# Spatial attention: one product of q and k over the places for both images of a pair

## The chip, the cores and the metric

The kernel runs on one core of a Trainium2 chip. A core has a matrix engine (TensorE), a vector engine (VectorE), a scalar engine (ScalarE), a general engine (GpSimd) and a queue processor (SyncE), which run beside each other and wait for each other by semaphores. The trace calls them PE, DVE, ACT, POOL and SP; PEld is TensorE's loading of weights, PE its matmuls. SBUF is the working memory of 128 partitions, PSUM the memory in which TensorE adds up its products. The metric is the device time of one execution in microseconds (us), lower is better.

## The reference, cut to what matters

The whole program is two layers on an image batch: a convolutional block with an attention in frequency and one in space, then a state space layer. The change concerns the spatial attention of the first layer:

```python
B, DIM, HEADS, H, W = (8, 128, 8, 128, 128)
...
q_s = qkv(q1_w, q1_b, q3_w, q5_w).reshape(b, HEADS, hd, h * w)
k_s = qkv(k1_w, k1_b, k3_w, k5_w).reshape(b, HEADS, hd, h * w)
v_s = qkv(v1_w, v1_b, v3_w, v5_w).reshape(b, HEADS, hd, h * w)
q_s = _l2norm_lastdim(q_s)
k_s = _l2norm_lastdim(k_s)
attn_s = jnp.einsum('bhcn,bhdn->bhcd', q_s, k_s) * temp_s[None]
attn_s = jax.nn.softmax(attn_s, axis=-1)
out_s = jnp.einsum('bhcd,bhdn->bhcn', attn_s, v_s).reshape(b, c, h, w)
```

Here qkv is a 1x1 convolution followed by grouped 3x3 and 5x5 convolutions. For each image and each of 8 heads, every one of 16 channels of q is multiplied with every one of 16 channels of k and summed over all 16384 places. That sum, before the norms, is what the change makes in another way.

## The kernel before, in words

The program runs in stages. First come group norm and the 1x1 convolutions, then the attention in frequency, then the spatial attention (lines 505 to 602), then a stage that mixes both (from line 610), and last the state space layer. Everything is in fp32.

The stage of the spatial attention takes the eight images in four pairs (loop over b, line 559). An image's channels are cut in four blocks (loop over blk, line 562), and each block holds 16 groups; a group is one step of the grouped convolutions.

conv (line 517) loads one quad of groups of both images into src (one of three buffers, issued from SyncE's queue, line 521) and makes it with 64 products of 32 by 32 weights by 512 columns into four PSUM tiles c_mm (line 529). What happens to a c_mm tile is decided by the function that is handed in. use_q squares it on ScalarE and writes it on VectorE twice into qm, once for each of two kinds of channels, with the other kind's partitions zeroed (lines 544 and 545). use_k squares it and copies it into kk (line 549). use_v copies it to vst and stores it.

qm has the shape 128 x (kind 2) x (group 16) x (image 2) x (place 256), and kk the shape 128 x (group 16) x (image 2) x (place 256). The partitions hold the position in an 8 by 8 patch and the channel of the group, and the last axis holds the patches. So neighbouring groups, read at one place, lie 512 words apart, and neighbouring images 256 words apart.

After the twelve calls of conv for q, v and k of a block comes the sum over the places. For each of the two images f, 256 products are made, one for each place n: the weights are 32 columns of qm (2 kinds by 16 groups), the moving data 16 columns of kk, both contracted over the 128 partitions. Product n goes to the PSUM partitions 32 j to 32 j + 31 with j = n modulo 4, so four partial sums run beside each other in the four column groups of the array. VectorE copies them out (gs, line 579), and one product with the constant sums4 adds the four partial sums into at (the tile c_at, line 581). Two further products (line 583) put the sums of squares beside it. qm, kk, the PSUM tile c_gram and the PSUM tile c_at have one buffer each.

Then conv makes the fourth kind, the convolution of x itself, for the block's groups (line 585), and the next block follows. After the four blocks the norms and the softmax of both images are worked out on VectorE and ScalarE (from line 586).

The order on each engine is set by a scheduler when the program is built. On TensorE it stands like this in a block: the 256 products of the first image, four products of the next conv, the one c_at product from gs and the two from sq, the 256 products of the second image, again four products of conv, the three c_at products, and then the rest of conv. In the trace every fp32 product shows as two pairs of a weight load and a matmul.

small is a constant of 128 columns, of which the first 82 are used. Its first 32 columns are sums4, and line 516 names its parts.

Of the kernel before, what the change touches and what calls it, by code (L numbers as in the profile page):

```python
# [9 lines left out]
F32 = mybir.dt.float32  # L10
# [8 lines left out]
NH, HD = 8, 16  # L19
# [26 lines left out]
def _constants():  # L46
    i = np.arange(128)
    ang = 2 * np.pi * np.outer(i, i) / 128
    cos, sin = np.cos(ang), np.sin(ang)
    block = (i[:, None] // HD == i[None, :] // HD).astype(np.float64)  # L50
    u = np.arange(1, 64)

    tc = np.concatenate([cos[:, 64:65], sin[:, u], cos[:, u], cos[:, 0:1]], 1)
    a1 = np.concatenate([cos[64:65], 2 * sin[u], 2 * cos[u], cos[0:1]], 0) / HW
    a2 = np.concatenate([cos[64:65], 2 * cos[u], -2 * sin[u], cos[0:1]], 0) / HW
    made = {
        "ident": np.eye(128),
        "group4": (i[:, None] // 4 == i[None, :] // 4) / 4.0,
        "mask": block,
        "neg": (block - 1) * 1e30,  # L60

        "c16": block * np.cos(2 * np.pi * np.outer(i, i) / HD) / HD,
        "s16": block * np.sin(2 * np.pi * np.outer(i, i) / HD) / HD,
        "first": block * (i[None, :] % HD == 0) / HD,

        "cmp": cos.reshape(128, 32, 4).transpose(0, 2, 1).reshape(128, 128),
        "smp": sin.reshape(128, 32, 4).transpose(0, 2, 1).reshape(128, 128),
        "tc": tc, "cm": cos, "sm": sin, "sneg": -sin, "a1": a1, "a2": a2,
    }


    kind, quarter = i // 16 % 2, i // 32
    made["blocks"] = (kind[:, None] == i[None, :] // 64) & (quarter[:, None] == i[None, :] // 16 % 4)
    small = np.zeros((128, 128))
    small[:, 0:32] = i[:, None] % 32 == i[None, :32]
    small[:, 32:64] = kind[:, None] == i[None, :32] // 16
    small[:, 64:80] = i[:, None] % 16 == i[None, :16]
    small[:, 80:82] = kind[:, None] == i[None, :2]
    made["small"] = small

    ker = np.exp(2j * np.pi * np.outer(np.arange(HW), i) / HW).mean(1)
    ker = ker[(128 * (i[None, None, :] - i[:, None, None]) + i[None, :, None]) % HW]
    ker = np.stack([-ker.imag, ker.real, ker.imag], 2)
    return (
        np.concatenate([made[n] for n in _CONSTS], 1).astype(np.float32),
        ker.astype(np.float32),
    )
# [6 lines left out]
def _layout(a):  # L94

    a = {n: np.asarray(v) for n, v in a.items()}
    o = {"x": np.ascontiguousarray(a["x"]).reshape(B, C, HW)}
    o["consts"], o["ker"] = _constants()
    p = "L0_conv_"
    f, s = a[p + "projf_w"].reshape(C, 2 * C), a[p + "projs_w"].reshape(C, 2 * C)  # L100
# [67 lines left out]
def tile_kernel(ctx: ExitStack, tc: tile.TileContext, I: dict, out: bass.AP):  # L168
    nc = tc.nc
# [25 lines left out]
    def const(name, n=1):  # L195
        i = _CONSTS.index(name)
        return cst[:, i * 128 : (i + n) * 128]
# [60 lines left out]
    with tc.tile_pool(name="a_x", bufs=4) as xp_, tc.tile_pool(name="a_p", bufs=5) as pp_, tc.tile_pool(  # L258
        name="a_t", bufs=2
# [3 lines left out]
        for b in range(B):  # L263
# [67 lines left out]
            for i in range(HW // px):  # L331
# [5 lines left out]
                n = rows if i else rows - 1  # L337
# [21 lines left out]
    with tc.tile_pool(name="b_x", bufs=1) as xp_, tc.tile_pool(name="b_g", bufs=1) as gp_, tc.tile_pool(  # L359
        name="b_w", bufs=3  # L360
# [18 lines left out]
        for b in range(B):  # L379
# [7 lines left out]
            for q in range(2):  # L387
# [10 lines left out]
                for k in range(4):  # L398
                    kk = 4 * q + k
# [6 lines left out]
            for u in range(5):  # L406
# [4 lines left out]
                for c0 in range(0, 13 * C, 512):  # L411
                    n = min(512, 13 * C - c0)
# [5 lines left out]
            gram = psum.tile([128, 512], F32, name="f_gram", tag="ps")  # L418
            for d in (1, 0):
# [5 lines left out]
                for v in range(64):  # L425
                    nc.tensor.matmul(  # L426
                        gram[:, :128], lhsT=xh[:, :, (W - 64 * d - v) % W], rhs=xr[:, :, v],
                        start=(d == 1 and v == 0), stop=(d == 0 and v == 63),
# [76 lines left out]
    with tc.tile_pool(name="c_w", bufs=1) as cw_, tc.tile_pool(name="c_qk", bufs=1) as qkp, tc.tile_pool(  # L505
        name="c_x", bufs=3
    ) as srcp, tc.tile_pool(name="c_v", bufs=6) as vp_, tc.tile_pool(name="c_s", bufs=2) as sp_, tc.tile_pool(
        name="c_ps", bufs=6, space=PSUM
# [4 lines left out]
                taps[:, 4 * i : 4 * i + 4].rearrange("p g c o m -> p (g c o m)"), I["taps"][:, i * 2048 : (i + 1) * 2048]  # L513
            )
        small = const("small")
        sums4, kinds, same16, ofkind = small[:, 0:32], small[:, 32:64], small[:, 64:80], small[:, 80:82]
        def conv(b, cv, gq, use):

            src = srcp.tile([128, 2, PL], F32, name="src")
            for f in range(2):  # L520
                nc.sync.dma_start(src[:, f, :], PQKVX[cv][b + f, 8 * gq : 8 * gq + 8].rearrange("c n s -> (c n) s"))
            grid = src.rearrange("p f (i j) -> p f i j", j=GR)
            banks = [psum.tile([128, 2, 256], F32, name="c_mm", tag="ps") for _ in range(4)]
            for o in range(4):
                for r in range(4):
                    rs = slice(32 * r, 32 * r + 32)
                    for s in range(4):
                        y0, x0 = 8 * s + o // 2, o % 2
                        nc.tensor.matmul(  # L529
                            banks[r][32 * s : 32 * s + 32].rearrange("p f (i j) -> p f i j", j=32),  # L530
                            lhsT=taps[rs, gq, cv, o, :], rhs=grid[rs, :, y0 : y0 + 8, x0 : x0 + 32],
                            start=(o == 0), stop=(o == 3),
                        )
            for r in range(4):
                use(cv, 4 * gq + r, banks[r])
# [23 lines left out]
        for b in range(0, B, 2):  # L559
            sq = sp_.tile([128, 2, 2, NG], F32, name="sq")  # L560
            at = gps_.tile([128, 2, 3, HD], F32, name="c_at")
            for blk in range(4):

                qm = qkp.tile([128, 2, HD, 2, 256], F32, name="qm")
                kk = qkp.tile([128, HD, 2, 256], F32, name="kk")
                for gq in range(4 * blk, 4 * blk + 4):
                    for cv, use in ((0, use_q), (2, use_v), (1, use_k)):
                        conv(b, cv, gq, use)
                for f in range(2):

                    gram = gps_.tile([128, HD], F32, name="c_gram")
                    for n in range(256):
                        j = n % 4
                        nc.tensor.matmul(  # L574
                            gram[32 * j : 32 * j + 32, :], lhsT=qm[:, :, :, f, n].rearrange("p a g -> p (a g)"),
                            rhs=kk[:, :, f, n], start=(n < 4), stop=(n >= 252),
                        )
                    gs = sp_.tile([128, HD], F32, name="gs")
                    nc.vector.tensor_copy(gs, gram)
                    js, gb = slice(32 * blk, 32 * blk + 32), slice(HD * blk, HD * blk + HD)  # L580
                    nc.tensor.matmul(at[js, f, 0], lhsT=sums4, rhs=gs, start=True, stop=True)
                    for n in range(2):
                        nc.tensor.matmul(at[js, f, 1 + n], lhsT=kinds, rhs=sq[:, f, n, gb], start=True, stop=True)
                for gq in range(4 * blk, 4 * blk + 4):
                    conv(b, 3, gq, use_v)
            for f in range(2):

                rn = sp_.tile([128, 2, HD], F32, name="rn")
                nc.scalar.activation(rn, at[:, f, 1:3], AF.Sqrt)
                nc.vector.tensor_scalar(rn, rn, L2_EPS, None, ALU.max)  # L590
                nc.vector.reciprocal(rn, rn)
                rq = sp_.tile([128, 1], F32, name="rq")
                nc.vector.tensor_tensor(rn[:, 0], rn[:, 0], same16, ALU.mult)
                nc.vector.tensor_reduce(rq, rn[:, 0], AX.X, ALU.add)
                a = sp_.tile([128, HD], F32, name="at_a")
                nc.vector.tensor_tensor(a, at[:, f, 0], rn[:, 1], ALU.mult)
                nc.vector.tensor_scalar(a, a, rq, cvec[:, 4:5], ALU.mult, ALU.mult)
                mx = sp_.tile([128, 1], F32, name="at_m")
                nc.vector.tensor_reduce(mx, a, AX.X, ALU.max, negate=True)
                sm = sp_.tile([128, 1], F32, name="at_sum")  # L600
                nc.scalar.activation(a, a, AF.Exp, bias=mx, accum_out=sm)
                nc.vector.reciprocal(sm, sm)
                nc.vector.tensor_scalar(aS[:, b + f, :], a, sm, None, ALU.mult)
# [6 lines left out]
    with tc.tile_pool(name="d_o", bufs=1) as op_, tc.tile_pool(name="d_v", bufs=2) as vp_, tc.tile_pool(  # L610
        name="d_k", bufs=3
    ) as kp, tc.tile_pool(
        name="d_w", bufs=3
# [3 lines left out]
        for b in range(B):  # L617
# [43 lines left out]
            n = H // RB  # L661
# [49 lines left out]
    with tc.tile_pool(name="e_c", bufs=1) as cp, tc.tile_pool(name="e_w", bufs=2) as wk, tc.tile_pool(  # L711
        name="e_h", bufs=4
    ) as hp, tc.tile_pool(name="e_d", bufs=3, space=DRAM) as dp, tc.tile_pool(
        name="e_b", bufs=2, space=PSUM
# [337 lines left out]
        for n in range(-2 * ST, (total + 1) * ST):  # L1052
            i, s = divmod(n, ST)
# [40 lines left out]
```

## The time and the profile before

| what | value |
|---|---|
| time, median of 3 runs | 21334.16 us (21333.18 to 21354.21) |
| time of the profiled execution | 21360.55 us |
| its span, first to last instruction | 21358.5 us |
| mean granted TensorE clock | 0.945 |
| PE busy in the span | 18573.9 us (87%) |
| DVE busy in the span | 13875.6 us (65%) |
| c_gram matmuls (line 574) | x16384, busy 450.6 us, 258 ns each |
| c_gram weight loads (line 574) | x16384, busy 442.6 us, 215 ns each |
| c_mm matmuls (line 529) | x32768, busy 1522.0 us, 657 ns each |
| gs copies (line 579) | x32, 174 ns each |

Engines overlap, so busy times do not add up to the span. The duration of a single matmul or load is a latency: many are in flight at once, and how often one starts is read from a count in a window of time. The chain of waits follows the work that ended last back through what released it, and shows which work lay on the path. An "issue" piece in it is time in which an engine waited for nothing that the profile shows. A row of a window gives the stretch, its length, then for each engine the busy time and the number of instructions, then the granted clock, the busy share of the DMA engines and GB/s.

### The profile page before, as it was taken

Reading aid. Unit: us, or ns where it says so; the run is one execution under the profiler, and the core shown is the slowest. Engines: PE = TensorE matmul, PEld = TensorE weight load, DVE = VectorE, ACT = ScalarE, POOL = GpSimd, SP = SyncE. Lnnn points to the kernel's source line nnn. Section 1 sums busy time; section 2 is a strip of 40 time slices with the busy share of each in tenths; the row PEclk is TensorE's granted clock in tenths of the full one; section 3 lists DMA queues with packets and bytes.
Section 4 is the critical chain, followed back from the end, with each engine's and each line's share of the span. In section 5 each row is a group of like instructions: output and inputs, shape, how many; then the busy total and the mean of one; then the engine's idle time right before and its main releaser. Section 6 shows DMA issues by size and latency. Waiting matters only on the chain.

```text
span 21358.5 us, 802425 instructions
## 1 busy us (share of the span) xinstructions
PE 18573.9 (87%) x360816; PEld 10741.9 (50%) x360816; DVE 13875.6 (65%) x14884; ACT 11748.4 (55%) x25436; POOL 11924.1 (56%) x7116
## 2 busy tenths in 40 slices
PE   5647889889998898988989999898998989989898
PEld 3335667644546565644444444444444444444444
DVE  3332111133332333379999999999999999999999
ACT  2222222222222221267777777777777777777777
POOL 2221000000001111178889889898888888989888
PEclk8878999988889999999999999999999999999999
DMA  9996333255557888854444444444444444444443
GB/s 275 277 278 171 82 82 77 67 201 195 194 193 218 235 228 237 226 109 97 94 102 96 99 97 95 103 96 100 95 95 101 96 100 96 98 101 96 103 96 84
DMA packets 2989828, 2929.13 MB, mean 137 GB/s; under 512 B 1480494, under 2 KB 2275630, under 8 KB 2981667
## 3 DMA queue, kind: packets, MB, share of 16 engines
q1 hardware_dynamic: 2274818, 2537.53, 46.9%
q10 hardware_dynamic: 672672, 206.02, 4.5%
q0 software_dynamic: 38912, 134.24, 2.0%
q8 instruction: 2842, 46.56, 0.9%
q14 instruction: 584, 4.78, 0.1%
HBM read 1975.21 MB, written 902.04 MB: 135 GB/s over the span
## 4 chain that ended last, share of the span: by engine, by line
PE 53%; DVE 19%; ACT 12%; DMA 8%; issue 6%; SPq 2%; POOL 1%; DVEq 0%; ACTq 0%; POOLq 0%
DVE hs L157 14%; PE hb L157 9%; PE c_mm L529 6%; PE y L157 4%; PE e_xc L157 4%; ACT dA L157 4%; ACT L157 4%; DVE bd L157 3%; DMA d_ls<-LS 2%; PE e_z L157 2%; PE x_q L471 2%; PE d_a L641 2%; PE f_gram L426 2%; PE c_gram L574 2%; PE a_mm L308 2%
## 5 line engine op out<-in xcount | busy, mean ns | idle before, releaser
L157 POOL TENSOR_TENSOR hc<-hs,crep 128x1024 f32<-128x1024 f32 x4096 | 9648.7, 2374 | 1308.3 <-DVE hs L157 808.1
L157 DVE TENSOR_TENSOR_SCAN hs<-dA,state,hb 128x512 f32<-128x512 f32 x7936 | 9584.5, 1263 | 854.3 <-PE hb L157 788.4
L157 PEld LDWEIGHTS hb<-bd,duT 64*32 64x32 f32 x262144 | 3749.3, 106 | 3751.0 <-issue 2769.6
L157 PE MATMUL hb<-bd,duT 64*32 64x128 f32 x262144 | 4925.4, 275 | 727.8 <-issue 507.7
L157 ACT ACTIVATE dA<-dlrep,A 128x512 f32<-128x512 f32 x8192 | 5443.4, 713 | 6.9 <-ACT state L157 0.8
L157 PE MATMUL e_xc<-u,wf 128*128 128x512 f32 x4096 | 2255.5, 644 | 412.1 <-ACT u L157 365.4
L656 POOL TENSOR_TENSOR sq<-sq 128x512 f32<-128x512 f32 x256 | 324.5, 1268 | 3269.8 <-ACT sq L655 3269.8
L157 PE MATMUL y<-hc,gath 128*32 128x512 f32 x16384 | 2090.2, 611 | 12.9 <-issue 11.4
L157 ACT COPY state<-hs 128x2 f32<-128x2 f32 x4096 | 776.6, 190 | 1903.4 <-DVE hs L157 1885.5
L529 PE MATMUL c_mm<-src,taps 32*32 32x512 f32 x32768 | 1522.0, 657 | 168.9 <-ACT junk L540 74.7
L157 ACT ACT_TABLE_LOAD x1023 | 1312.5, 1283 | 346.1 <-PE e_dt L157 287.6
L493 POOL DMA_DIRECT2D OFL<-ya x128 | 113.6, 887 | 2448.2 <-ACT ya L490 2448.2
L529 PEld LDWEIGHTS c_mm<-src,taps 32*32 32x32 f32 x32768 | 636.0, 107 | 992.2 <-issue 399.7
L157 ACT ACTIVATE bd<-same,bt 128x64 f32<-128x64 f32 x4096 | 1054.6, 339 | 29.6 <-PE hb L157 29.3
L157 PEld LDWEIGHTS e_xc<-u,wf 128*128 128x128 f32 x4096 | 650.7, 193 | 835.3 <-ACT u L157 425.2
L157 DVE TENSOR_TENSOR bd<-same,e_bt 128x512 f32<-128x512 f32 x1536 | 1023.3, 666 | 0.0
L460 DVE TENSOR_TENSOR pr<-x_x,G 128x512 f32<-128x512 f32 x256 | 264.9, 1035 | 1127.5 <-PE x_x L456 1127.5
L232 ACT ACTIVATE gn_sd<-gn_gv,eps 128x1 f32<-128x1 f32 x16 | 4.2, 261 | 1741.6 <-PE gn_gv L230 1741.6
L642 DVE COPY pq<-d_a 128x512 f32<-128x512 f32 x512 | 354.1, 692 | 930.8 <-PE d_a L641 930.8
L308 PE MATMUL a_mm<-xt,wp 128*128 128x256 f32 x3072 | 746.6, 397 | 91.4 <-ACT pv L315 56.1
L554 ACT COPY vst<-c_mm 128x512 f32<-128x512 f32 x256 | 149.8, 585 | 1222.4 <-PE c_mm L529 908.2
L695 DVE TENSOR_TENSOR x<-d_p,d_x 128x512 f32<-128x512 f32 x256 | 276.0, 1078 | 822.7 <-PE d_p L692 718.4
(198 smaller groups left out, 22965.9 us busy)
## 6 DMA issues: line engine op xcount, KB each, us to landing
dlrep<-dld SPq DMA_DIRECT2D x2048, 256.0 KB
crep<-cd SPq DMA_DIRECT2D x2048, 128.0 KB
ker<-in_ker SPq DMA_DIRECT2D x256, 768.0 KB
dld<-dl SPq DMA_DIRECT2D x256, 512.0 KB
src<-Pq SPq DMA_DIRECT2D x128, 544.5 KB
src<-Pv SPq DMA_DIRECT2D x128, 544.5 KB
src<-Pk SPq DMA_DIRECT2D x128, 544.5 KB
src<-Px SPq DMA_DIRECT2D x128, 544.5 KB
```

The lines of the kernel that those rows point to most:

```text
L157: made = method(*args, **kwargs)
L308: nc.tensor.matmul(ps[:, y : y + 2], lhsT=weight("qkv"[n]), rhs=now, start=True, stop=True)
L426: nc.tensor.matmul(gram[:, :128], lhsT=xh[:, :, (W - 64 * d - v) % W], rhs=xr[:, :, v], start=(d == 1 and v == 0), stop=(d == 0 and v == 63),)
L460: nc.vector.tensor_tensor(pr.rearrange("p c (t s) -> p c t s", t=2), xs.rearrange("p c (t s) -> p c t s", t=2), gate, ALU.mult)
L471: nc.tensor.matmul(qp[:, c], lhsT=pr[:, 2 * i + c, :], rhs=const("cmp", 2).rearrange("p (t w) -> p t w", t=2), start=True, stop=True,)
L529: nc.tensor.matmul(banks[r][32 * s : 32 * s + 32].rearrange("p f (i j) -> p f i j", j=32), lhsT=taps[rs, gq, cv, o, :], rhs=grid[rs, :, y0 ...
L554: nc.scalar.copy(o, ps)
L574: nc.tensor.matmul(gram[32 * j : 32 * j + 32, :], lhsT=qm[:, :, :, f, n].rearrange("p a g -> p (a g)"), rhs=kk[:, :, f, n], start=(n < 4), ...
L641: nc.tensor.matmul(ps[:, r, :], lhsT=xn[:, j + r, :], rhs=aF[:, b, :], start=True, stop=True)
L642: nc.vector.tensor_copy(pq[:, j : j + 2, :], ps)
L656: nc.gpsimd.tensor_tensor(sq[:, :, 0, :], sq[:, :, 0, :], sq[:, :, 1, :], ALU.add)
L695: nc.vector.tensor_tensor(nat[0], ps.rearrange("p (y e j) -> p y e j", y=4, e=4), nat[1], ALU.add)
```

## The change

The loop over the two images no longer encloses the sum over the places. One sum of 256 products serves both images. Its weights are 64 columns of qm (2 kinds by 16 groups by 2 images) and its moving data 32 columns of kk (16 groups by 2 images). Product n goes to the PSUM partitions 64 j to 64 j + 63 with j = n modulo 2, so there are two partial sums in two halves of the array instead of four in four quarters. The result holds also the products of one image's q with the other image's k, which nothing reads.

One copy of 128 x 32 brings the sums to gs. Inside the loop over f, the product with a constant picks the rows of image f and adds the two partial sums, while gs[:, :, f] picks the columns of image f. That takes two constants instead of sums4: the columns 0 to 31 and 82 to 113 of small. The first columns now also mark other rows. The two products from sq are as before.

In the built order of TensorE a block has the 256 wider products, four products of the next conv, then the three c_at products of the first image and the three of the second, and the rest of conv.

```diff
@@ _constants
-    small[:, 0:32] = i[:, None] % 32 == i[None, :32]
+    for f in range(2):
+        small[:, 82 * f : 82 * f + 32] = i[:, None] % 64 == 2 * i[None, :32] + f
...
@@ tile_kernel
-        sums4, kinds, same16, ofkind = small[:, 0:32], small[:, 32:64], small[:, 64:80], small[:, 80:82]
+        sums, kinds, same16, ofkind = (small[:, 0:32], small[:, 82:114]), small[:, 32:64], small[:, 64:80], small[:, 80:82]
...
+                gram = gps_.tile([128, HD, 2], F32, name="c_gram")
+                for n in range(256):
+                    j = n % 2
+                    nc.tensor.matmul(
+                        gram[64 * j : 64 * j + 64], lhsT=qm[:, :, :, :, n].rearrange("p a g f -> p (a g f)"),
+                        rhs=kk[:, :, :, n], start=(n < 2), stop=(n >= 254),
+                    )
+                gs = sp_.tile([128, HD, 2], F32, name="gs")
+                nc.vector.tensor_copy(gs, gram)
                 for f in range(2):
-                    gram = gps_.tile([128, HD], F32, name="c_gram")
-                    for n in range(256):
-                        j = n % 4
-                        nc.tensor.matmul(
-                            gram[32 * j : 32 * j + 32, :], lhsT=qm[:, :, :, f, n].rearrange("p a g -> p (a g)"),
-                            rhs=kk[:, :, f, n], start=(n < 4), stop=(n >= 252),
-                        )
-                    gs = sp_.tile([128, HD], F32, name="gs")
-                    nc.vector.tensor_copy(gs, gram)
                     js, gb = slice(32 * blk, 32 * blk + 32), slice(HD * blk, HD * blk + HD)
-                    nc.tensor.matmul(at[js, f, 0], lhsT=sums4, rhs=gs, start=True, stop=True)
+                    nc.tensor.matmul(at[js, f, 0], lhsT=sums[f], rhs=gs[:, :, f], start=True, stop=True)
```

## The prediction

> **What bounds the kernel now.** I read the page's slices first, then the chain of waits inside the stage that the change touches, then that stage's products by tile and by window. The stage of the spatial attention runs from 4314.7 to 6516.0 us, a tenth of the span. In it TensorE is the engine that sets the pace: a window over the stage shows it busy 1977.14 of 2201.30 us, VectorE 707.24 and ScalarE 552.53. The chain over one sum and its surroundings, in order of time (start, us, what):
>
> ```profile
> 4392.39 0.70 DVE kk L549
> 4393.09 0.04 issue
> 4393.14 10.07 PE c_gram L574 x248
> 4403.20 0.12 issue
> 4403.32 3.22 PE c_gram L574 x91
> 4406.54 0.53 issue
> 4407.07 0.72 PE c_gram L574 x9
> 4407.79 0.99 PE c_mm L529 x8
> 4408.79 0.17 PE c_at L581 x2
> 4408.95 0.10 PE c_at L583 x3
> 4409.05 15.18 PE c_gram L574 x357
> 4424.22 0.99 PE c_mm L529 x8
> 4425.21 0.17 PE c_at L581 x2
> 4425.38 0.13 PE c_at L583 x4
> 4425.51 3.21 PE c_mm L529 x82
> ```
>
> The two sums of a block are on the path from end to end, nothing lies beside them, and what follows waits for TensorE. So every nanosecond saved or added there counts once. Two small stops lie in it: "issue" holes inside a sum, and the stretch between the sums, filled with eight conv pairs while the copy gs and the c_at products go through.
>
> How long a sum takes, by windows over six of them (us, busy us and count per engine, granted clock, DMA):
>
> ```profile
> 4393.13:4407.80 14.67, 14.02 (x512) 13.63 (x512) 0.00 (x0) 0.77 0.20 78
> 4408.87:4424.22 15.35, 15.35 (x512) 15.25 (x512) 0.00 (x0) 0.56 0.02 4
> 4528.38:4543.28 14.90, 14.85 (x512) 14.63 (x512) 0.00 (x0) 0.54 0.20 77
> 4545.20:4559.74 14.54, 14.54 (x512) 14.43 (x512) 0.00 (x0) 0.50 0.02 5
> 4665.81:4680.18 14.37, 13.43 (x512) 13.01 (x512) 0.00 (x0) 0.63 0.21 81
> 4682.10:4695.28 13.18, 12.55 (x512) 12.25 (x512) 0.00 (x0) 0.83 0.02 5
> ```
>
> A sum of 256 products is 512 pairs of a weight load and a matmul (fp32 takes two pairs for each product). Together the six take 87.01 us, 14.5 us each, 28.3 ns for a pair. The reader should see that the clock hardly matters: 14.54 us at 0.50, 14.67 at 0.77. TensorE's own arithmetic is therefore not what limits a pair. What does? Two whole-array products of the stage before tell (chain, and groups by form):
>
> ```profile
> 1893.21 28.23 PE f_gram L426 x128
> ```
>
> ```profile
> L426 PEld LDWEIGHTS f_gram<-xr,xh 128*128 128x128 f32 x2048 | 447.5, 311 | 199.3 <-issue 177.6 <-DMA xr<-XR 21.7
> ...
> L444 PEld LDWEIGHTS x_y<-cst,xh 128*128 128x128 f32 x2048 | 280.0, 200 | 108.9 <-issue 107.1
> ```
>
> Both load 128 columns and stream 128. x_y reads neighbouring words; eight of its pairs take 0.89 us at full clock (window 2653.14 to 2654.03), 111 ns each. f_gram reads words that lie 512 and 256 bytes apart; 128 pairs take 28.23 us, 220 ns each, and its load lasts 311 ns against 200. Scattered words cost twice as much, about 1.7 ns a column (220 / 128). c_gram reads words 2048 bytes apart.
>
> **What the skill says.** "TensorE: Matmul & The Clock Gate", section "LDWEIGHTS (loading the stationary operand)": a load takes its columns divided by 1.2, in ns, whatever the depth: 27, 53 and 107 ns for 32, 64 and 128. x_y's 111 agrees, f_gram's 220 does not. "Advanced Engine Details and Errata", section "Memory Cachelines", has the reason: lines of 16 bytes in SBUF, and full speed needs at least two hits on a line. f_gram's factor of two agrees. "TensorEngine Tiling (Array Packing)", section "Tiling Modes": 128 rows by 32 columns are four independent tiles, 128 by 64 only two. "Runtime: NRT & Kernel Launch", section "Instruction fetch mechanics": instructions come in blocks of 256, a crossing is mostly hidden. Here it isn't quite: 128 pairs, then a hole of 0.42 to 0.73 us, is a pattern of the fast sums.
>
> **The change part by part**, for one block of 16 (four pairs of images by four blocks).
>
> 1. Fewer pairs: 2 x 512 become 512. At 28.3 ns this removes 14.5 us if a pair kept its price.
>
> 2. Dearer pairs. A load takes 64 scattered columns instead of 32, a matmul streams 32 instead of 16, into two column tiles instead of four. At f_gram's price a load of 64 takes 64 x 1.72 = 110 ns. Loads of one tile follow each other; two tiles work at once, so a pair cannot come more often than every 55 ns. The stream of 32, 55 ns per tile, fits beside the next load, as f_gram's does. 512 x 55 = 28.2 us, against 2 x 14.5 = 29.0: 0.8 us won. No trace shows a pair of this shape. Bounds: from below 28.3 ns (a pair costs what it does now, whatever its columns), from above 82 ns (load and stream of a tile, 110 + 55, one after the other, over two tiles). I take 55, because the same limit holds for both widths: columns read per pair double as pairs halve.
>
> 3. Instruction holes go, since 128 pairs at 55 ns last 7 us instead of 3.6. They are part of the 28.3 ns, so nothing more is counted.
>
> 4. The stretch between the sums goes: 1.07, 1.92 and 1.92 us in three windows, 1.6 on average. Its eight c_mm pairs move behind the sum (128 of them take 5.50 us at 4373.07, so 0.34 us for eight). Its two c_at and four sq pairs move too, 0.27 us in the chain. Net 1.0 us won.
>
> 5. One gs copy of 32 columns instead of two of 16 (174 ns each). The remaining one lies, as now, beside the eight c_mm pairs before c_at in the built order. The constant "small" grows within its 128 columns, so no DMA grows. The order of ScalarE is unchanged; on SP two d_vs loads of a later stage change places. Nothing. If the cover of eight c_mm went, the copy would cost 0.2 us a block.
>
> 6. Transfers: TensorE leaves the sums at most a little earlier. The three src buffers fill within the first sum (DMA share 0.20, then 0.02), so the conv after it finds its input in every case.
>
> Sum: 0.8 + 1.0 = 1.8 us a block, times 16, 29 us won. The profiled execution took 21360.55 us (span 21358.5), 26 us above the median of 21334.16; the same saving on the median gives 21305 us, 0.14% less. A change within 0.2%, 43 us, is about what cannot be told from none.
>
> **The rivals.** The break-even price of a pair is (29.0 + 1.0) / 512 = 58.6 ns, close to my 55, so both signs are near.
>
> - *Shared reading.* Four tiles at f_gram's price would allow 32 x 1.72 / 4 = 14 ns a pair, yet the best 128 pairs in a row (3.05 us at 5075.47) need about 22. If that is a limit on words read by all tiles together, and one tile may go faster than f_gram did, doubling gives 44 ns: 22.5 us, 7.5 a block with the stretch, 120 us, 21214. For it: the clock's indifference. Against: f_gram's 311 ns load, which had one tile and no crowd.
> - *A pair keeps its price*, by issue or by fetching. 14.5 + 1.0 us a block, 248 us, 21086. For it: the holes after 128 pairs. Against: hb pairs come 128 in 2.03 us (10187.43), so issue allows 16 ns, and f_gram's loads scale with columns.
> - *Loads and streams of a tile get in each other's way* (the slow side). Now a tile's turn is 4 x 22 = 88 ns at best where the load alone needs 55: something stretches it, 1.6 times. With half the tiles there is less to overlap. If the stretch is 1.3 at 64 columns, a pair costs 71.5 ns: 36.6 us, 6.6 lost a block, 106 us, 21440. Wholly in series, 82 ns, 42.0 us, 12 lost a block, 192 us, 21526. It decides from 58.6 ns on. For it: 55 + 27 ns in series over four tiles is 20.5, near the 22 seen. Against: f_gram overlaps the two.
>
> **How the numbers follow.** Same work, 55 ns: 0.38, own range 21275 to 21350; a twentieth of all lies in its part below 21291. Shared reading 0.23, price kept 0.09, in each other's way 0.30, of which 0.02 stays within 43 us. Faster 0.05 + 0.23 + 0.09 = 0.37; slower 0.28; same 0.35. The likeliest is the first: 21305. The range takes it in with shared reading and the milder half of the slow rival, 21180 to 21450; left out are the kept price (0.09) and the serial end (about 0.11).
>
> **What would show it.** The windows over c_gram should have 512 pairs in about 28 us per block; 23 or 15 would speak for the first or second rival, 36 or more for the third. A load of c_gram should last some 50 ns longer than the median of 207. The holes of about 0.5 us and the wait of VectorE's gs on c_gram (492.0 us over 32 times) should turn to about 28 us each, 16 times. The prediction is wrong if conv products cost something else in the changed kernel, since nothing here touches them.

## The result, and the profile after

The changed kernel takes 21528.15 us (median of 5 runs, 21510.79 to 21544.07) against 21334.16 us before (5 runs, 21314.86 to 21354.21). The ratio is 1.009, with a 95% interval of 1.0078 to 1.0101: slower by 194 us. The forecast was 29 us faster, and the range ended at 21450.

The profiled execution of the changed kernel took 21521.16 us (span 21519.4). Its chain of waits over one block of the stage (start, us, what):

```profile
4395.63 0.70 DVE kk L550
4396.33 0.04 issue
4396.37 43.59 PE c_gram L575 x508
4439.96 1.86 PE c_mm L530 x8
4441.82 0.22 PE c_at L583 x2
4442.04 0.21 PE c_at L585 x4
4442.25 0.11 PE c_at L583 x2
4442.36 0.21 PE c_at L585 x4
4442.57 5.43 PE c_mm L530 x95
```

The two sums with eight conv pairs between them, 32.1 us from 4393.14 to 4425.21 before, are now one unbroken piece of 43.59 us. The "issue" holes inside the sum and the stretch between the sums are gone, as forecast. What is left is one number: the price of a pair. Four of the sixteen sums, by windows over the tile c_gram (start and end, length, busy us and count for TensorE, its weight loads and VectorE, then clock, DMA share, GB/s):

```profile
4396.37:4439.96 43.59, 43.59 (x512) 43.45 (x512) 0.00 (x0) 0.50 0.07 25
4545.82:4588.57 42.75, 42.74 (x512) 42.62 (x512) 0.00 (x0) 0.51 0.07 26
4693.33:4739.12 45.79, 45.78 (x512) 45.67 (x512) 0.00 (x0) 0.50 0.06 24
6045.00:6083.60 38.60, 38.59 (x512) 38.45 (x512) 0.00 (x0) 0.50 0.08 29
```

512 pairs stand in each window. From the first start to the last, the sixteen sums take 43.0 us on average, 84 ns a pair, where 55 was forecast. By the same measure, a sum of this one kernel lies anywhere between 38.3 and 45.8 us. The tile's own view shows the same from the other side:

```profile
L575 PEld LDWEIGHTS c_gram<-kk,qm x8192: 197/283/336, 4396.4 to 6678.5; 128*64 128x64 f32 x200
L575 PE MATMUL c_gram<-kk,qm x8192: 305/367/434, 4396.4 to 6678.5; 128*64 128x32 f32 x200
...
  PE c_gram L575: 695.4, 16
```

A load lasts 283 ns in the median instead of 207, 76 longer where some 50 were expected. VectorE's wait before gs is 695.4 us over 16 times, 43.5 each, and was 492.0 over 32.

Where the time came from: a block, from its first c_gram pair to the conv that follows, grew from 32.85 to 45.90 us on average, which makes 209 us over sixteen. The stage, from the first to the last start of c_mm, grew from 2193.6 us (4314.8 to 6508.4) to 2399.7 us (4318.1 to 6717.8), 206 us. So the whole loss lies in the sums. The two spans differ by less, 161 us, because the later stages, whose code is the same, took 48.5 us less in this execution, and the stage began 3.3 us later. No cause for that is shown; runs of the kernel before lay 39 us apart here and 59 us in a later group. The medians stand at 194.

### The profile page after: what moved, and what is told of

Read it like the earlier page. It is cut to its first block, busy times and chain, and to the rows that moved or that the text cites. A ratio compares the mean times of both kernels' runs of the same rounds, so it can differ in the third digit from the quotient of the medians.

```text
span 21519.4 us, 786027 instructions
## 1 busy us (share of the span) xinstructions
PE 18754.3 (87%) x352624; PEld 10976.8 (51%) x352624; DVE 13872.6 (64%) x14868; ACT 11748.1 (55%) x25436; POOL 11926.6 (55%) x7116
## 4 chain that ended last, share of the span: by engine, by line
PE 54%; DVE 18%; ACT 12%; DMA 7%; issue 6%; SPq 2%; POOL 1%; ACTq 0%; DVEq 0%; POOLq 0%
DVE hs L158 14%; PE hb L158 9%; PE c_mm L530 5%; PE y L158 4%; PE e_xc L158 4%; ACT L158 4%; ACT dA L158 4%; PE c_gram L575 3%; DVE bd L158 3%; DMA d_ls<-LS 2%; PE e_z L158 2%; PE x_q L472 2%; PE d_a L643 2%; PE f_gram L427 2%; PE a_mm L309 2%
## 5 line engine op out<-in xcount | busy, mean ns | idle before, releaser
L530 PE MATMUL c_mm<-src,taps 32*32 32x512 f32 x32768 | 1492.5, 655 | 170.9 <-ACT junk L541 72.5
```

What stands on the lines that cost most here:

```text
L530: nc.tensor.matmul(banks[r][32 * s : 32 * s + 32].rearrange("p f (i j) -> p f i j", j=32), lhsT=taps[rs, gq, cv, o, :], rhs=grid[rs, :, y0 ...
```

## The experiments

The kernel before took between 21219 and 21334 us from one group of runs to the next, so each run is compared with it in its own group, on the same chip: 21219.29 us (one run) for the first four kernels below, 21321.06 us (one run) for the two with offsets or distance, swapped, and by place, and 21242.72 us (median of 7, 21215.03 to 21274.14) for both, and for the three with rows of 260 words. Most were run once, so their totals say little below some 60 us, the scatter of the kernel before. What they are judged by is the pace of the pairs, read from windows over c_gram or from the starts of its pairs.

**Is it the width, or the number of column groups?** The kernel before, with its pairs of 32 and 16 columns unchanged, put into two groups of the array, or into one:

```diff
# e1_two_groups
-                        j = n % 4
+                        j = n % 2
...
# e2_one_group
-                        j = n % 4
+                        j = n % 1
```

(The conditions for start and stop, and the rows of gs, gram and sums4, follow the number of groups.)

> The kernel before with its sums made in two column groups (32 columns each) instead of four; the result is the same. Theory 1, in series: in one column group the load of scattered words and the stream of scattered words follow each other, 55 + 27 = 82 ns, so two groups give 41 ns a pair, 21 us a sum instead of 14.5. Theory 2, shared reading: all groups together are held by the words read, so the pair stays at 22 to 28 ns while the load alone (57 ns over two groups, 28.5 ns) allows it: about 14.6 us a sum. Theory 3, a crowd of groups stretches each load: with two groups the stretch goes, 28.5 ns as in theory 2, and a load of c_gram lasts near 133 ns instead of 207.

> The kernel before with its sums made in one column group of 32; the result is the same. Theory 1, in series: 82 ns a pair, 42 us a sum. Theories 2 and 3: the stream lies beside the next load, so the load alone sets the pace, 57 to 60 ns, 30 us a sum.

The windows over one sum, first with two groups, then with one:

```profile
4302.50:4325.20 22.70, 22.65 (x512) 22.55 (x512) 0.00 (x0) 0.50 0.13 49
```

```profile
4301.50:4335.30 33.80, 33.67 (x512) 33.56 (x512) 0.09 (x1) 0.50 0.08 31
```

Two groups give 42.8 ns a pair on average and 21463.10 us in all, one group 65.5 ns and 21858.98 us. So the kernel before loses just by using two groups instead of four, and twice 42.8 is 86, close to the changed kernel's 84 for a pair of twice the columns. The granted clock is not the reason: the sums stand at 0.50 here, but one of the kernel before that also stood at 0.50 (4545.20 in the prediction) took 14.54 us. The group that works alone takes 65.5 ns, less than load and stream one after the other (82) and more than the load alone (55): the serial mechanism of the third rival falls, though its price came near.

**Which reading costs it, the load's or the stream's?** The changed kernel with the same number of words, but 64 neighbouring words as weights, or 32 neighbouring words as moving data (the sums are then made from other words; only the changed part of each line is shown):

```diff
# e3_flat_weights
-   lhsT=qm[:, :, :, :, n].rearrange("p a g f -> p (a g f)"),
+   lhsT=qm.rearrange("p a g f n -> p (a g f n)")[:, 64 * n : 64 * n + 64],
...
# e4_flat_moving
-   rhs=kk[:, :, :, n],
+   rhs=kk.rearrange("p g f n -> p (g f n)")[:, 32 * n : 32 * n + 32].rearrange("p (g f) -> p g f", f=2),
```

> The changed kernel with the 64 columns of weights read from neighbouring words of qm (other words than the sum needs, so the sums are others); the stream stays scattered. The changed kernel takes 43.0 us for its sum, 84 ns a pair. Theory 1, in series: 53 + 55 = 108 over two groups, 54 ns, 28 us a sum. Theories 2 and 3, stream beside load: 55 ns at most in a group, 28 to 30 ns a pair, 15 us a sum.

> The changed kernel with the 32 moving columns read from neighbouring words of kk (other words than the sum needs); the weights stay scattered. Theory 1, in series: 110 + 27 = 137 over two groups, 68 ns, 35 us a sum. Theories 2 and 3: the load of 110 ns sets the pace, 55 to 58 ns, 28 to 30 us a sum.

Two windows with flat weights:

```profile
4300.74:4328.20 27.46, 27.46 (x512) 27.39 (x512) 0.00 (x0) 0.50 0.10 38
4572.80:4592.60 19.80, 19.79 (x512) 19.74 (x512) 0.00 (x0) 0.91 0.15 57
```

Flat weights bring the pair to 53.3 ns at a clock of 0.50 and 38 ns at 0.91 (total 21174.96). Flat moving data bring it to 71.6 ns (total 21281.62). Both readings have a part in it, and neither alone explains it. The prices lie near the 54 and 68 ns that the serial reading expected, but the single group has just spoken against that reading. What the two kernels share is that something scattered remains while the other reading has left its place.

**Does it matter where in memory the readings meet?** In the changed kernel every word of one product lies a multiple of 1024 bytes from the next, so all 96 words of a product n lie at the same place of any shorter power of two (if both tiles begin at such a place too, which no view shows; the offsets below bear it out). Two kernels move readings apart without changing their kind. The first lets each block read kk at another place than qm. The second keeps the places of a product and gives the two groups places that are d apart, instead of neighbours. The first makes products of other words, the second the same products in another order:

```diff
# e6_offsets
+                off = [0, 1, 2, 4, 8, 16, 32, 64, 128, 3, 12, 24, 48, 96, 0, 192][2 * b + blk]
...
-                            rhs=kk[:, :, :, n], start=(n < 2), stop=(n >= 254),
+                            rhs=kk[:, :, :, (n + off) % 256], start=(n < 2), stop=(n >= 254),
...
# e7_distance
-                for n in range(256):
-                    j = n % 2
+                d = [1, 2, 4, 8, 16, 32, 64, 128, 1, 2, 4, 8, 16, 32, 64, 128][2 * b + blk]
+                for m in range(256):
+                    j = m % 2
+                    n = m // 2 // d * 2 * d + m // 2 % d + d * j
```

> The changed kernel, but each of its 16 sums reads the moving data from another place than the weights, kk at n + off with off = 0, 1, 2, 4, 8, 16, 32, 64, 128, 3, 12, 24, 48, 96, 0, 192 in the order of the sums (the sums are others than the reference's). So far: one group of 32 columns takes 65.5 ns a pair, more than its load (55) and less than load and stream in series (82), so neither theory 1 nor plain overlap holds. Theory 4, same place: load and stream read words at the same place n and so the same part of the memory of a partition, and wait for each other; with some offsets the wait goes, and these sums fall from 43 us to the 28 to 30 us of the load alone, 55 to 58 ns, while offsets below 4 (the same 16 bytes) stay at 43. Theory 3, a crowd, whatever the addresses: all sixteen stay at 38 to 46 us.

> The changed kernel with its 256 places in another order; the result is the same but for rounding. The two column groups work on places d apart instead of 1, with d = 1, 2, 4, 8, 16, 32, 64, 128 in the sums 0 to 7 and again in 8 to 15. Theory 4: groups meet in the same part of the memory too; from some d on the pair falls from 84 ns to the 65.5 ns turn of one group, extended to 64 columns (131 over two groups, 65 ns, 33 us a sum). Theory 3: no sum changes, 43 us.

Windows of the first, with the stream 0, 4, 32 and 64 words from the load:

```profile
4350.67:4393.60 42.93, 42.92 (x512) 42.78 (x512) 0.00 (x0) 0.50 0.07 25
...
4800.53:4838.60 38.07, 38.07 (x512) 37.97 (x512) 0.00 (x0) 0.51 0.08 29
...
5233.70:5271.10 37.40, 37.36 (x512) 37.23 (x512) 0.00 (x0) 0.51 0.08 30
5381.10:5424.90 43.80, 43.78 (x512) 43.64 (x512) 0.00 (x0) 0.50 0.07 26
```

Of the second, with the groups 2, 4, 16 and 64 places apart:

```profile
4509.07:4552.40 43.33, 43.32 (x512) 43.32 (x512) 0.00 (x0) 0.50 0.07 27
4662.58:4695.40 32.82, 32.81 (x512) 32.75 (x512) 0.00 (x0) 0.50 0.09 33
4942.44:4975.20 32.76, 32.76 (x512) 32.76 (x512) 0.00 (x0) 0.50 0.07 29
5217.80:5264.80 47.00, 47.00 (x512) 46.94 (x512) 0.00 (x0) 0.51 0.06 23
```

| words apart | 0 | 1 | 2 | 3 | 4 | 8 | 12 to 48 | 64 | 96 | 128 | 192 |
|---|---|---|---|---|---|---|---|---|---|---|---|
| stream from load, ns a pair | 83 | 81.5 | 83.5 | 77.9 | 73.9 | 72.5 | 72.5 | 85.0 | 72.5 | 84.2 | 83.0 |
| group from group, ns a pair | – | 86 to 89 | 85 | – | 63.7 | 63.8 | 63.8 (16 and 32) | 92 | – | 90 | – |

The pattern repeats after 64 words, 256 bytes: 64, 128 and 192 are as bad as 0, and 96 is as good as 32. Inside the period, 4 words, 16 bytes, are nearly enough. The distance of the groups is worth 20 ns, as expected; that of the stream from the load 11, where 26 to 29 were expected.

**Do the two add up to the whole loss?** One kernel takes the four combinations in its four blocks (with an offset, the sums are made from other words):

```diff
# e8_both
+                d, off = [(1, 0), (1, 8), (16, 0), (16, 8)][blk]
...
+                            rhs=kk[:, :, :, (n + off) % 256], start=(m < 2), stop=(m >= 254),
```

> The changed kernel with two settings for each of its 16 sums, in turn over the four blocks: distance d between the places of the two column groups and offset off of the moving data's place from the weights', (1, 0), (1, 8), (16, 0), (16, 8); with an offset the sums are others than the reference's. The two runs before gave 83, 72.5 and 63.8 ns a pair for the first three alone. Theory 4, same place: with both apart nothing meets, and the fourth reaches the pace of the load alone, 55 ns (28 us a sum), which is what the prediction had taken. Theory 3, a crowd whatever the addresses: the fourth stays at 63 or above.

Windows over the four blocks of the first pair of images:

```profile
4299.53:4344.75 45.22, 45.21 (x512) 45.07 (x512) 0.00 (x0) 0.50 0.06 24
4449.38:4486.75 37.37, 37.36 (x512) 37.23 (x512) 0.00 (x0) 0.50 0.08 30
4596.03:4628.90 32.87, 32.86 (x512) 32.77 (x512) 0.00 (x0) 0.50 0.09 34
4738.77:4767.10 28.33, 28.33 (x512) 28.25 (x512) 0.00 (x0) 0.51 0.10 39
```

81 to 88 ns with neither, 72.5 and 63.8 with one, and 55.0 with both, the same in all four rounds. 55.0 is the price that the prediction took for the load alone, and 28.33 us about the length that it took for a sum. The four settings differ only in which words are read when, at the same clock, so between 84 and 55 lies nothing but where the readings lie. That the load holds the 55.0 is not shown by this: at this clock flat weights took 53.3, hardly less.

**The remedy without a change of what is read.** If rows of qm and kk are 260 words long instead of 256, the words of one product step through the period by 16 bytes (by 32 in the kernel before, which reads every second row):

```diff
-                qm = qkp.tile([128, 2, HD, 2, 256], F32, name="qm")
-                kk = qkp.tile([128, HD, 2, 256], F32, name="kk")
+                qm = qkp.tile([128, 2, HD, 2, 260], F32, name="qm")
+                kk = qkp.tile([128, HD, 2, 260], F32, name="kk")
```

(The three writes by VectorE go to [..., 0:256].) This was put into the changed kernel (p1) and into the kernel before (p3):

> The changed kernel with rows of 260 words instead of 256 in qm and kk; the result is the same. Neighbouring columns then lie 1040 bytes apart, one 16-byte line further in the period of 256 bytes that the offsets showed, so loads and streams no longer stay in one place of it. Theory 4: no more than 55 to 58 ns a pair, 28 to 30 us a sum instead of 43, time near the kernel before. If the doubled price of scattered words also comes from staying in one place, a load is as quick as a flat one: still 53 ns at half clock, 27 to 35 ns at full. If every new line costs, whatever its place, 55 ns at either clock.

> The kernel before with rows of 260 words in qm and kk; the result is the same. The load alone allows 32 x 1.72 / 4 = 14 ns a pair, so if the places alone held it at 28, the sum falls to 7 to 8 us and the time by 200 us. If the fetching of instructions, 128 pairs in about 3.5 us, is the next limit, the sum stays at 13 to 14 us and the time within 30 us of the kernel before.

A sum of the changed kernel in a window, then the sum of one image of the kernel before in TensorE's timeline (start, us, instructions, and in brackets the idle time ahead of them):

```profile
4308.39:4338.95 30.56, 30.53 (x512) 30.40 (x512) 0.00 (x0) 0.50 0.10 38
```

```profile
4301.14 4.20 PE L574 MATMUL c_gram<-kk,qm 128*32 128x16 f32 x242 [2.73 <-DVE kk L549]
4306.75 2.26 PE L574 MATMUL c_gram<-kk,qm 128*32 128x16 f32 x128 [1.42 <-issue]
4310.50 2.24 PE L574 MATMUL c_gram<-kk,qm 128*32 128x16 f32 x128 [1.49 <-issue]
4314.25 0.47 PE L574 MATMUL c_gram<-kk,qm 128*32 128x16 f32 x14 [1.51 <-issue]
```

The changed kernel comes to 59.2 ns a pair in every sum and 21268.25 us, 26 above the kernel before and inside that one's scatter: nearly the whole loss is gone. The kernel before runs its pairs at 16.1 ns in stretches (median of its unbroken runs of 128 pairs, which lie between 15.6 and 16.8), where it took 27.2 between its few holes. But now holes stand between these stretches, 1.4 to 1.5 us here and between 1.1 and 1.8 in most sums, so 26.0 ns remain over a sum, and the time is 21223.53, 19 less and inside the scatter as well. So its pace between holes was held by meetings too. The holes fit the instruction fetching that the prediction named, which no run tests apart.

**The change with four groups.** One sum for both images needs not have 64 weight columns. With the parts exchanged, kk gives 32 weight columns and qm 64 moving ones, in four groups:

```diff
# v1_swapped
-                    j = n % 2
+                    j = n % 4
...
-                        gram[64 * j : 64 * j + 64], lhsT=qm[:, :, :, :, n].rearrange("p a g f -> p (a g f)"),
-                        rhs=kk[:, :, :, n], start=(n < 2), stop=(n >= 254),
+                        gram[32 * j : 32 * j + 32], lhsT=kk[:, :, :, n].rearrange("p g f -> p (g f)"),
+                        rhs=qm[:, :, :, :, n], start=(n < 4), stop=(n >= 252),
...
-                    nc.tensor.matmul(at[js, f, 0], lhsT=sums[f], rhs=gs[:, :, f], start=True, stop=True)
+                    nc.tensor.matmul(at[js, f, 0], lhsT=gs[:, :, :, f].rearrange("p a g -> p (a g)"), rhs=sums[f], start=True, stop=True)
```

> One sum for both images with the parts exchanged: 32 columns of kk are the weights, in four column groups, and 64 columns of qm move; the result is the same. As many words are read as in the changed kernel. If the number of groups is what was lost (theories 1 and 3), a pair costs half of 84 ns, 41 to 45 ns, 21 to 23 us a sum, and the time falls about 100 us below the kernel before. If the words alone count (theory 2), the sum stays at 43 us.

> The exchanged parts (32 columns of kk as weights in four groups, 64 columns of qm moving) with rows of 260 words; the result is the same. Without the rows a pair cost 54.5 ns. If scattered words in different places are as quick as flat ones, four groups at full clock allow (53 + 4) / 4 = 14 ns, and the blocks of 256 instructions hold it at about 27 ns: 14 us a sum, 240 us below the kernel before. If each scattered word keeps its double price, 110 / 4 = 28 ns gives the same 14 us.

A window of the swapped kernel, two of the swapped kernel with rows of 260 words (p2), and the chain of the latter:

```profile
4361.08:4388.40 27.32, 27.29 (x512) 26.87 (x512) 0.00 (x0) 0.94 0.08 29
```

```profile
4299.57:4315.40 15.83, 15.79 (x512) 15.52 (x512) 0.00 (x0) 0.90 0.18 67
4419.29:4435.10 15.81, 15.81 (x512) 15.54 (x512) 0.00 (x0) 0.90 0.18 71
```

```profile
4299.57 15.79 PE c_gram L575 x496
4315.37 0.99 PE c_mm L530 x8
```

Swapped alone, a pair takes 54.5 ns (41 to 45 were expected, so this was missed: four groups at one place do not work twice as fast as two) and the kernel 21205.92 us, 115 below the one before in one run each. With both, a pair takes 30.4 ns in the median sum, a sum 15.6 us on average, and the kernel 20970.08 us (median of 4, 20962.42 to 20990.22). Against the 21242.72 of before the ratio is 0.987, interval 0.9854 to 0.9887. It beats both kernels. Only one hole, of 0.72 us, stands in its sixteen sums: 128 of its pairs last 3.9 us, longer than the 3.7 that 128 take together with their hole in p3 (2.24 + 1.49).

**Another layout.** The last kernel lays qm and kk out by place, so that a product reads neighbouring words and VectorE's writes are scattered:

```diff
# v2_by_place
-                qm = qkp.tile([128, 2, HD, 2, 256], F32, name="qm")
-                kk = qkp.tile([128, HD, 2, 256], F32, name="kk")
+                qm = qkp.tile([128, 256, 2, HD, 2], F32, name="qm")
+                kk = qkp.tile([128, 256, HD, 2], F32, name="kk")
```

> The changed kernel with qm and kk laid out by place, so that the weights and the moving data of a product are neighbouring words, and the scattered words are written instead, by VectorE; the result is the same. Flat weights gave 53.3 ns at half clock and about 35 at full clock; with both flat I expect 53 ns at half clock, 27 to 29 ns at full, so 15 to 27 us a sum instead of 43. VectorE's writes (743 and 692 ns each now) may get dearer: at twice the time the stage would lose about 400 us, at the same time it gains 250 to 450 us on the changed kernel.

One of its windows over c_gram, and one of its writes to qm by tile (ns least/median/most):

```profile
4524.80:4552.30 27.50, 27.50 (x512) 27.39 (x512) 0.00 (x0) 0.50 0.08 31
```

```profile
L545 DVE TENSOR_SCALAR qm<-c_mm,cst x256: 1039/1106/1157, 4301.1 to 6511.1; 128x512 f32<-128x512 f32 x128
```

The pair falls to 52.7 ns, but the write rises from a median of 743 to 1106 ns. The total is 21398.62, 78 above the kernel before in one run each. With rows of 260 words (p1) the same write keeps its 743 ns.

**The runs in one table.** The kernels read one word per column and partition, so a pair of 32 and 16 columns reads 48, one of 64 and 32 reads 96. A block reads the same number in both kernels, 1024 x 48 = 512 x 96.

| kernel | groups | words a pair | ns a pair | words a ns | for each group |
|---|---|---|---|---|---|
| one group (e2) | 1 | 48 | 65.5 | 0.73 | 0.73 |
| two groups (e1) | 2 | 48 | 42.8 | 1.12 | 0.56 |
| changed | 2 | 96 | 84 | 1.14 | 0.57 |
| before | 4 | 48 | 28.3 | 1.70 | 0.42 |
| swapped (v1) | 4 | 96 | 54.5 | 1.76 | 0.44 |
| changed, rows of 260 (p1) | 2 | 96 | 59.2 | 1.62 | 0.81 |
| changed, both apart (e8) | 2 | 96 | 55.0 | 1.75 | 0.87 |
| before, rows of 260, between holes (p3) | 4 | 48 | 16.1 | 2.98 | 0.75 |
| swapped, rows of 260 (p2) | 4 | 96 | 30.4 | 3.16 | 0.79 |

The upper five read at one place of the period: each group gets less the more groups there are, but four together still get half as much again as two. There the width of a pair does not matter (e1 against changed, before against swapped). The lower four spread their words, and a group gets 0.75 to 0.87 words a ns. That this is one limit is not shown. The 16.1 ns of p3 are also about the pace of hb, another small product, whose 128 pairs took 2.03 us in the prediction, and p1 and e8 stand at a clock of 0.50. f_gram, one group of 128 columns, reads 256 words in 220 ns, which is 1.16 a ns. What is shown is that the change kept the words and halved the groups, at one place of the period.

## Why the prediction was wrong, point by point

- **Step 2, dearer pairs**, failed, and the miss is all in it: 55 ns were taken and 84 measured. 512 x (84 − 55) ns = 14.8 us a block, 238 us over sixteen, against 223 between forecast and result. The 110 ns for a load of 64 agree with the 55.0 of e8, but that was measured at half clock, where flat weights take 53.3 as well, so they are not proved. What failed is the sentence that the stream "fits beside the next load, as f_gram's does", together with the two tiles taken as independent. Load, stream and the two groups read the same place of a 256-byte period and hold each other up. Parting the load from the stream gave 11 ns, parting the groups 20, both 29.
- *Why f_gram was no guide.* Its product v reads xr at place v and xh at place −v (counted in the 64 words of the period, from the start of each tile), so its load and stream meet in two of 64 products alone, v = 0 and v = 32. The trace of before shows it there: of the 128 loads of a pass nearly all last 310 ns, but the second load of v = 0 takes 371 to 374 and that of v = 32 takes 381 to 387, in each of the sixteen passes over v. The first view is of the products up to v = 31 of one pass, the second of those around v = 32 (ns least/median/most):

```profile
L426 PEld LDWEIGHTS f_gram<-xr,xh x60: 310/310/311, 1893.9 to 1906.7; 128*128 128x128 f32 x60
L426 PEld LDWEIGHTS f_gram<-xr,xh x5: 310/315/384, 1906.7 to 1907.6; 128*128 128x128 f32 x5
```

- The reason given, "the same limit holds for both widths", was half true. Where places and groups are kept, words do set the price. But the limit was not a load's time over the number of groups: the kernel before stood at 28.3 ns where its load alone allows 55 / 4 = 14. The prediction saw this gap ("something stretches it, 1.6 times") and gave it to the slow rival only, although it was also the best clue to the likeliest case. Had the stretch of before been carried over, the price would have been above the break-even of 58.6 ns.
- **Steps 1, 3 and 4** came as said. Half the pairs are issued, the holes are gone, and so is the stretch between the sums: the block grew by 13.05 us where the sums alone, from the first start to the last end, grew by 43.36 − 2 x 14.53 = 14.3, so 1.25 us was won, near the forecast net of 1.0. Two of its terms were off, in opposite directions. The stretch between the sums was 1.76 us on average, not 1.6. The eight conv pairs behind the sum take 1.86 us, where step 4 priced them at 0.34 and its own chain already showed 0.99.
- **Step 5** holds: the one gs copy takes 191 ns and lies beside those eight pairs. **Step 6** holds: the DMA share is 0.07 in the sums, and conv follows the c_at products at once. The conv products cost no more than before, c_mm being busy 1492.5 us against 1522.0.
- *Shared reading* (44 ns) was wrong in price, but close in kind: readings of several tiles do share something. It is a place of memory, not a total.
- *A pair keeps its price* (28 ns) is refuted: pairs of these 96 words took between 55.0 and 92 ns in two groups by their places alone, and 30.4 in four groups with the parts exchanged (p2).
- *Loads and streams in each other's way* had the sign, and its end at 82 ns gave 21526, almost the result. That the number fits so well is in part luck, since its mechanism is only the smaller part of the loss: one group alone takes 65.5 ns, not 82, so load and stream overlap in part even when they meet, and more than half of the loss lies between the two groups.
- The point from which it decides, 58.6 ns, stood the test: with 59.2 ns a block of the changed kernel (p1) takes 33.08 us to the conv that follows, where 32.85 stood before.

Left open: why four groups at one place still read half as much again as two, why the price of the changed kernel wanders between 70 and 91 ns from one stretch of 128 pairs to the next, and whether the 55.0 ns would fall at a higher clock. The swapped kernel (v1) won more than its sums and the stretch can give: its block to the conv that follows takes 29.61 us against 32.85, 52 us over sixteen blocks, of 115 in all. The c_mm matmuls were busy 1442.1 us in it against 1522.0 before, which could hold part of the rest but was not tested apart, and the totals are single runs.

## What to carry to other kernels

Before making small products wider, count how many column groups remain and where their words lie: with strides of 1024 and 2048 bytes, multiples of the 256-byte period that the offsets showed, load, stream and neighbouring groups met at one place, and halving the groups cost half again as much for the same words. A row longer by 16 bytes cut the price of a pair by two fifths with four groups, and by three tenths with two. Before taking another product's overlap as a guide, see whether its load and stream meet. Where a measured pair is slower than its load alone allows, price the wider one by what stretches the narrow one, not by the load.

## What the runs showed of the hardware that was not expected

- Readings of one partition by TensorE collide with a period of 256 bytes and a grain of about 16: 83 to 85 ns a pair at 0, 64, 128 or 192 words between load and stream, 72.5 at 8, 16, 32 or 96.
- TensorE counted as busy throughout, and still its granted clock stood at 0.50 in the changed kernel's sums (32 moving columns). With 64 moving columns in four groups it was 0.89 to 0.95 (p2, v1). Two sums with flat weights had 0.91 with 32 columns too, so the width is not the whole reason, which stays open.
- At that half clock, flat weights save nothing over scattered ones that meet nobody: 53.3 ns against 55.0. At 0.91 they take 38.
- Once pairs come every 16.1 ns (p3), most stretches of 128 are followed by a hole, 1.4 us in the median and about three in a sum. The kernel before, at 27.2 ns between holes, had one of 0.2 to 1.0 us in a sum.
